# Score products of an attention stage on four 64x64 tiles of TensorE

## The chip, the cores and the metric

The kernel runs on one core of a Trainium2 chip. Its time is device time in microseconds (us) for the whole program. TensorE is called PE, VectorE DVE, ScalarE ACT, GpSimd POOL; SP is the queue that only issues DMAs. The program is written in a tile framework: it allots buffers from pools, puts the instructions of each engine into an order, and sets the semaphores between them.

## The reference

Four preactivation layers follow each other, each `x = x + f(group_norm(x))`. The change lies in the first, an axial attention over the 64 positions of one axis. With 4 images, 64 rows each, 16 groups of heads and 64 positions:

```
qkv = bn(einsum('nci,oc->noi', xp, w_qkv))          # n: image and row, i: position
q, k, v = qkv[:, :, :8], qkv[:, :, 8:16], qkv[:, :, 16:]      # per group g
qe = einsum('ngci,cij->ngij', q, q_emb)             # position terms of the query
ke = einsum('ngci,cij->ngij', k, k_emb)             # and of the key
qk = einsum('ngki,ngkj->ngij', qe, ke)              # their product: the scores
sim = bn(concat([qk, qe, ke]))                      # statistics over n, i, j
sim = softmax(sum of the three, axis=3)
out = einsum(sim, v), einsum(sim, v_emb) -> bn -> sum of the two
```

The batch norm of `sim` needs mean and variance of `qk`, `qe` and `ke` over all rows and positions before any softmax. Layers 2 to 4 are 3x3 convolutions (ternary weights; binary activations in two steps; weights built from a sigmoid form). They aren't touched.

## The kernel before

**Stage one** (L166 to L361) normalises the images, forms q, k and v (`po` at L284, `pv` at L299) and the sums for the first batch norm (`bn_stats` on DVE, squares on ACT, summed by PE in `psv`, L218). ACT copies q and k from PSUM into the two SBUF tiles `qs` of an image; after an image's last block, 16 DMAs on the SP queue (L326 to L331) write them to `q_d` in HBM.

**Stage two** (L389 to L667) makes the scores. It goes over 32 *pairs*: 4 images `b` times 8 pairs of groups `gp`. Before the loop, `et` is loaded on SP, and a chain of eight steps (`ptb` and `prs`, L410 to L414) makes the constants `tb` and `rsum` from it. Two pairs share one set `qb` (`projections(j)`: eight DMAs of 128 KB on SP; `scaled`: four DVE operations, L441). Each pair has two halves of its rows (`nb`), and each half two halves of the positions (`jh`). In one such quarter:

- `position_terms` (L466 to L486): 32 fp32 matmuls `pd` on eight 64x32 tiles (each matmul is two records in the profile, 64 for the block), into two PSUM buffers of `psd`; two DVE transposes (L483) bring them into the tiles `t0`, `t1`.
- `finish`, twice, for the half *before*: `product` (L488 to L504) does 16 fp32 matmuls `pq` of 64x64x64 on the tiles (0,0) and (64,64), into one PSUM bank; ACT copies it into the score tile `o` with a running sum (L499), then squares it in PSUM with another sum (L504). `finish` also issues the DMAs of the pair before (`qk_d`, on ACT's queue).

So a pair has four `pd` blocks and eight `product` calls of 32 records each. After each pair `term_sums` (L446 to L464) makes the statistics of `qe` and `ke`: three small DVE steps over q for the means (L451 to L453), four matmuls `ptq` (L456) and four DVE multiply-and-sum operations (L461) for the squares.

The pools set the order: `psd` has three buffers of two banks, which `pd` (two) and `ptq` (one) share; `psq` has two of one bank; `t0` and `t1` have two each, `o` two, `qb` five, loaded three ahead. Beside the pairs, ten weight jobs of later layers run, mostly on DVE: `weights_3` (L511 to L526) six times and `weights_2` (L528 to L553) four times; the framework puts them early in the stage. After the last pair, L601 to L608 finish the products and write the last scores, and L614 to L634 make the statistics from `acc` (products) and `esum` (terms).

**Stage three** (from L671) loads the scores back, applies the softmax and multiplies with v: `e` (L794), `exp` (L834), `pa` (L872), `den` (L845), `pe` (L897, 128x32 tiles). Its constants `vb` and `ve` are loaded on SP at its start. Then come the convolutions, with the chip's longest matmul lines (L993, L1284, L1378).

Of the kernel before, what the change touches and what calls it, by code (L numbers as in the profile page):

```python
# [18 lines left out]
P = 128  # L19
# [22 lines left out]
def network(ctx: ExitStack, tc, x, wqkv, relm, relt, relw, relv, counts, masks, vecs, rowv, ab, w1, l2w1, l2w2, l3w, mats, out):  # L42
# [10 lines left out]
    def scratch(name, shape):  # L53
        return dram.tile(shape, F32, name=name, tag=name)

    q_d = [scratch(f"q_d{b}", [GP, 8, 2, 2, 8, 512]) for b in range(B)]
    vt_d = [scratch(f"vt_d{b}", [4, 2, P, GP, 16, 8]) for b in range(B)]
    qk_d = [scratch(f"qk_d{b}", [GP, P, HW]) for b in range(B)]

# [106 lines left out]
    with ExitStack() as ph:  # L166
# [12 lines left out]
        st1 = sp.tile([P, 2, B * NB, 6], F32, name="st1")  # L179
        mx = sp.tile([P, 2, B], F32, name="mx")  # L180

        def normalised(b):
# [87 lines left out]
        for b in range(B):  # L270
            xs, gm, rs = ready
            qs = [qp.tile([P, 8, 8, 64], F32, name=f"qs{t}_{b}", tag="qs") for t in range(2)]
            for k in range(NB):
# [49 lines left out]
                if k in (3, 7) and 2 * b + k // 4 - 1 in range(len(pieces)):  # L323
                    i = 2 * b + k // 4 - 1
                    pieces_1[i] = weights_1(i, "wb")
            for t in range(2):  # L326
                for l in range(8):
                    nc.sync.dma_start(
                        out=q_d[b][:, l, t].rearrange("a r c f -> (r c) a f"),
                        in_=qs[t][:, EIGHT[l]].rearrange("p a h -> p (a h)"),  # L330
                    )  # L331
        while squares:
            add_squares()

        mv1 = small(sp, [P, 4, 2])
# [53 lines left out]
    with ExitStack() as ph:  # L389
        rp = pool(ph, "b_r")  # L390
        bqps += [pool(ph, f"b_q{i}") for i in range(3, 5)]
        tp_ = pool(ph, "b_t", 2)
        op = pool(ph, "b_o", 2)
# [8 lines left out]
        nc.sync.dma_start(out=rm, in_=relm)  # L402
        et = rp.tile([64, 8, P], F32, name="et")
        nc.sync.dma_start(out=et, in_=relt)
# [16 lines left out]
        sq = spread_scales(sp, psq, xs1, M_TKC, False, "pq")  # L421
        acc = sp.tile([P, 2, GP, B * 8], F32, name="acc")
        esum = sp.tile([P, 2, G, 2 * B], F32, name="esum")

        def projections(j):

            b, s = divmod(j, 4)
            q = bqps[j % 5].tile([P, 4, 8, 64], F32, name=f"qb_{j}", tag="qb")
# [17 lines left out]
        def term_sums(j, q, half):  # L446

            b, s = divmod(j, 4)
            gs, ks, col = slice(4 * s, 4 * s + 4), slice(4 * half, 4 * half + 4), 2 * b + half
            m = jp.tile([P, 4, 4], F32, name=f"m_{j}_{half}", tag="m")  # L450
            nc.vector.tensor_reduce(m, q[:, :, ks], AX.X, ALU.add)  # L451
            nc.vector.tensor_tensor(m, m, rsum[:, ks].unsqueeze(1).to_broadcast([P, 4, 4]), ALU.mult)
            nc.vector.tensor_reduce(esum[:, 0, gs, col], m, AX.X, ALU.add)  # L453
            ps = psd.tile([P, 4, 4, 64], F32, name=f"ptq_{j}_{half}", tag="pd")
# [4 lines left out]
            for g in range(4):  # L459
                junk = jp.tile([P, 4, 64], F32, name=f"pr_{j}_{half}_{g}", tag="pr")  # L460
                nc.vector.scalar_tensor_tensor(  # L461
                    junk, ps[:, :, g], 1.0, q[:, g, ks], ALU.mult, ALU.mult,
                    accum_out=esum[:, 1, 4 * s + g, col : col + 1],
                )  # L464

        def position_terms(q, ts, gp, nb, jh, name):  # L466
            pds = [psd.tile([P, 4, 32, 8], F32, name=f"pd_{name}_{t}_{jh}", tag="pd") for t in range(2)]
            for m in range(4):
                for g in range(2):
                    for kh in range(2):  # L470
                        for t in range(2):
                            rows = slice(64 * t, 64 * t + 64)
                            c = 2 * g + kh
                            a = 4 * kh + m
# [12 lines left out]

        def product(ts, o, k, col, gp, name):  # L488

            ps = psq.tile([P, 8, 64], F32, name=f"pq_{name}_{k}", tag="pq")  # L490
            for m in range(8):
                n = 8 * (k % 4) + m
                for g in range(2):
                    rows = slice(64 * g, 64 * g + 64)
                    nc.tensor.matmul(  # L495
                        ps[rows, m, :], lhsT=ts[1][rows, n // 2, :, n % 2], rhs=ts[0][rows, n // 2, :, n % 2],
                        start=True, stop=True, tile_position=(64 * g, 64 * g),
                    )
            nc.scalar.activation(  # L499
                o[:, :, 8 * k : 8 * k + 8, :], ps.rearrange("p n (a b) -> p a n b", b=2), AF.Copy,  # L500
                accum_out=acc[:, 0, gp, col : col + 1],
            )
            psf = ps.rearrange("p n i -> p (n i)")
            nc.scalar.activation(psf, psf, AF.Square, accum_out=acc[:, 1, gp, col : col + 1])  # L504

# [22 lines left out]
        def weights_2(i, g):  # L528

            w = kp.tile([P, 9, 64], F32, name=f"w2_{i}_{g}", tag="w2")  # L530
            if i == 0:
# [5 lines left out]
            w3 = w.rearrange("p k o -> p (k o)").rearrange("p (a n) -> p a n", a=3)  # L537
            u = kp.tile([P, 4, 3 * 64], F32, name=f"u2_{i}_{g}", tag="u2")
            t = kp.tile([P, 3 * 64], F32, name=f"t2_{i}_{g}", tag="t2")
# [20 lines left out]
        def finish(step, k):  # L560
            ts, o, b, gp, nb = step
            product(ts, o, 4 * nb + k, 8 * b + 4 * nb + k, gp, f"{b}_{gp}")

            if whole:
# [6 lines left out]
                if part == 3:  # L571
                    whole.pop()
            if nb == 1 and k == 3:
# [39 lines left out]
        tot = small(sp, [P, 2, GP])  # L613
        nc.vector.tensor_reduce(tot, acc, AX.X, ALU.add)  # L614
# [1203 lines left out]
```

## Time and profile before

| | |
|---|---|
| time, median of 3 runs | 2853.01 us (2845.20 to 2862.32) |
| time of the profiled execution | 2858.52 us |
| its span | 2856.7 us |
| PE busy | 2485.8 us (87%) |
| DVE busy | 1975.4 us (69%) |
| ACT busy | 1227.1 us (43%) |
| first `pd` of stage two | 287.3 us |
| last `pq` of stage two ends | 963.3 us |
| stage two's `pq`, busy over the whole span | 278.8 us, 8192 records |
| stage two's `pd`, likewise | 284.8 us, 8192 records |
| stage two's transposes, likewise | 304.1 us, 256 |

Busy time is an average over stages that are bound by different engines, so a stage has to be read from its own window. In a line of the groups, "128*32" or "64*64" is the part of the PE array that an instruction takes (rows x columns), the numbers behind it partitions x elements; "idle before" is what the engine waited ahead of this group, with the engine and line that ended the wait, and "issue" means that it waited for nothing that the profile shows. A PE record in the timeline overlaps the next, so paces are taken from start to start. PEld is the loading of a matmul's stationary operand, which runs beside PE.

### The profile page before, as it was taken

To read this page: it belongs to the slowest core of one execution; us is meant where nothing else is said; L and a number is where in the kernel's file an instruction comes from. 1 tells how busy PE (TensorE), PEld (TensorE's weight loads), DVE (VectorE), ACT (ScalarE), POOL (GpSimd) and SP (SyncE) were. 2 spreads that over 40 slices of the span, in tenths; PEclk is the share of its full clock that TensorE was granted. 3 is DMA by queue.
4 is the path that set the end of the run, shared out by engine and by line. 5 is a ranking of instruction groups with operands and counts; after the bars stand their busy time and mean duration, and the time that the engine had idled before them with its cause. 6 is when DMAs were issued, how large, how long until landed. Compare 5 with 4: busy or idle time off the path is not lost. (4 is left out here: it accounts for less than half of the span.)

```text
span 2856.7 us, 78236 instructions
## 1 busy us (share of the span) xinstructions
PE 2485.8 (87%) x34632; PEld 1675.3 (59%) x34632; DVE 1975.4 (69%) x3442; ACT 1227.1 (43%) x2240; POOL 96.3 (3%) x185
## 2 busy tenths in 40 slices
PE   7999889899999787888874789899998859999997
PEld 4566556667777566666764567677455424444443
DVE  6554997666666456666557878986888967958732
ACT  4554444555555555455533554653448521110100
POOL 0000000000000000000000000000000000000000
PEclk9999999999999799989997899999999979999998
DMA  6867466455544777777767546434436752333110
GB/s 241 256 204 217 137 192 161 126 128 130 145 109 104 181 255 258 263 255 248 258 216 231 167 165 198 163 132 171 132 116 242 279 196 92 118 117 134 45 45 31
DMA packets 257435, 489.71 MB, mean 171 GB/s; under 512 B 25984, under 2 KB 142336, under 8 KB 236352
## 3 DMA queue, kind: packets, MB, share of 16 engines
q1 hardware_dynamic: 184864, 292.32, 31.6%
q10 hardware_dynamic: 58336, 125.85, 15.8%
q0 software_dynamic: 13888, 66.46, 5.9%
q8 instruction: 274, 4.49, 0.6%
q14 instruction: 73, 0.60, 0.1%
HBM read 281.39 MB, written 203.16 MB: 170 GB/s over the span
## 5 line engine op out<-in xcount | busy, mean ns | idle before, releaser
L993 PE MATMUL gc<-gtr,g_u 128*128 128x512 f32 x1152 | 504.1, 599 | 13.8 <-DVE pc_o L1390 7.1
L993 PEld LDWEIGHTS gc<-gtr,g_u 128*128 128x128 f32 x1152 | 219.6, 192 | 290.1 <-issue 270.2
L483 DVE STREAM_TRANSPOSE t<-pd 128x1024 f32<-128x1024 f32 x256 | 304.1, 1226 | 114.6 <-PE pd L476 114.4
L476 PE MATMUL pd<-rm,qb 64*32 64x256 f32 x8192 | 284.8, 386 | 48.0 <-DVE t L483 41.3
L495 PEld LDWEIGHTS pq<-t,t 64*64 64x64 f32 x8192 | 259.1, 135 | 74.6 <-issue 50.8
L495 PE MATMUL pq<-t,t 64*64 64x64 f32 x8192 | 278.8, 220 | 18.7 <-issue 15.7
L499 ACT ACTIVATE o<-pq 128x512 f32<-128x512 f32 x256 | 152.1, 595 | 316.9 <-PE pq L495 311.2
L1378 PE MATMUL pc<-e_tr,e_k 128*64 128x512 bf16 x2304 | 264.9, 391 | 19.6 <-DVE e_tr L1367 13.0
L1284 PE MATMUL dc<-dh,d_u 128*128 128x512 f32 x768 | 235.3, 416 | 34.5 <-ACT dh L1261 34.5
L834 ACT ACTIVATE pt<-pt,sm 128x512 f32<-128x512 f32 x256 | 162.1, 709 | 170.8 <-DVE pt L804 170.7
L476 PEld LDWEIGHTS pd<-rm,qb 64*32 64x32 f32 x8192 | 157.0, 107 | 131.0 <-DVE t L483 59.6
L1284 PE MATMUL dc<-dl,d_u 128*128 128x512 f32 x768 | 230.7, 410 | 1.2 <-DVE dl L1262 1.1
L1378 PEld LDWEIGHTS <-e_k 128*64 128x64 bf16 x2304 | 144.9, 112 | 136.5 <-issue 27.4
L1284 PEld LDWEIGHTS dc<-dh,d_u 128*128 128x128 f32 x768 | 149.5, 196 | 75.8 <-ACT dh L1261 36.4
L804 DVE TENSOR_TENSOR pt<-e_False,si_False 128x1024 f32<-128x1024 f32 x128 | 151.6, 1216 | 35.1 <-PE e_False L794 34.0
L1284 PEld LDWEIGHTS dc<-dl,d_u 128*128 128x128 f32 x768 | 146.7, 193 | 43.6 <-DVE dl L1262 5.3
L1011 ACT COPY gc_c<-gc 128x512 f32<-128x512 f32 x32 | 18.6, 580 | 344.5 <-PE gc L993 324.5
L794 PE MATMUL e_False<-qc_False,rw 32*128 32x256 f32 x1024 | 129.7, 472 | 32.6 <-DVE pt L804 17.6
L504 ACT ACTIVATE pq<-pq 128x512 f32<-128x512 f32 x256 | 149.8, 585 | 3.9
L284 PE MATMUL po<-xg,wt 128*128 128x512 f32 x256 | 121.0, 611 | 6.5 <-DVE st L291 4.9
L299 PE MATMUL pv<-wt,xg 128*128 128x256 f32 x512 | 119.7, 382 | 0.0
L897 PE MATMUL pe_False<-pt,ve 128*32 128x64 f32 x4096 | 88.2, 238 | 34.5 <-issue 26.2
(396 smaller groups left out, 3611.0 us busy)
## 6 DMA issues: line engine op xcount, KB each, us to landing
si_False<-qk_d SPq DMA_DIRECT2D x64, 1024.0 KB
qk_d<-o ACTq DMA_DIRECT2D x124, 512.0 KB
x<-x_d SPq DMA_DIRECT2D x32, 1056.0 KB
xa<-in_x SPq DMA_DIRECT2D x16, 1024.0 KB
vt_d<-vs ACTq DMA_DIRECT2D x32, 512.0 KB
q_d<-qs SPq DMA_DIRECT2D x64, 256.0 KB
qb<-q_d SPq DMA_DIRECT2D x128, 128.0 KB
qc_False<-q_d SPq DMA_DIRECT2D x64, 256.0 KB
```

The source lines that it names most:

```text
L284: nc.tensor.matmul(psf, lhsT=wt[:, t, bass.ts(o, P)], rhs=xg[:, t, :], start=(t == 0), stop=(t == 1))
L476: nc.tensor.matmul(pds[t][32 * c : 32 * c + 32, m].rearrange("p j k -> p (j k)"), lhsT=q[rows, 2 * (gp % 2) + g, a, 32 * nb : 32 * nb + 32 ...
L483: nc.vector.transpose(ts[t][:, :, 32 * jh : 32 * jh + 32].rearrange("p a j b -> p j a b"), pds[t].rearrange("p m j k -> p j m k"),)
L495: nc.tensor.matmul(ps[rows, m, :], lhsT=ts[1][rows, n // 2, :, n % 2], rhs=ts[0][rows, n // 2, :, n % 2], start=True, stop=True, tile_posi ...
L499: nc.scalar.activation(o[:, :, 8 * k : 8 * k + 8, :], ps.rearrange("p n (a b) -> p a n b", b=2), AF.Copy, accum_out=acc[:, 0, gp, col : co ...
L504: nc.scalar.activation(psf, psf, AF.Square, accum_out=acc[:, 1, gp, col : col + 1])
L794: nc.tensor.matmul(es[x_ // 2][:, x_ % 2, :, :, par], lhsT=rw[rows, 63 - i : 127 - i].rearrange("p j r -> p (j r)"), rhs=q[rows, :, par, k ...
L804: nc.vector.tensor_tensor(dst, e, src, ALU.add)
L834: nc.scalar.activation(s, s, AF.Exp, scale=s2q[:, gp : gp + 1])
L993: nc.tensor.matmul(ms[k], lhsT=u[t][:, dx, k, bass.ts(co, P)], rhs=vs[t][:, k, :, dx : dx + 64], start=(first and dx == 0), stop=(last and ...
L1284: nc.tensor.matmul(at[k], lhsT=u[t][:, dx, k, bass.ts(co, P)], rhs=v[:, k, :, dx : dx + 64], start=(first and p_ == 0 and dx == 0), stop=( ...
L1378: nc.tensor.matmul(m[64 * g : 64 * g + 64], lhsT=parts[:, g, i, k, dx, :], rhs=vs[g][:, k, 8 * (q % 2) : 8 * (q % 2) + 8, dx : dx + 64], s ...
```

## The change

`product` now handles both halves of a pair's rows in one call and alternates between all four 64x64 tiles: half `nb` reads its terms from partitions 64*(g^nb) and writes its result to partitions 64*g, into a PSUM bank of its own. For that `position_terms` puts half 1 into exchanged partitions, and the products of a pair follow one whole pair behind its terms (`t0`, `t1` have four buffers each). A pair has four `product` calls of 64 records, each followed by two ACT copies out of PSUM and one ACT square over 128x1024, read from the score tile `o` in SBUF into a bf16 buffer that nobody reads. The three DVE steps for the q means leave `term_sums`. In their place, stage one sums each image's `qs` with two reductions over 128x4096, adds the four images up, and sends the result through HBM (`qs_d`: 16 DMAs on POOL's queue, four loads on SP) to a tile `qtot` of stage two; seven small DVE operations at the end of stage two turn it into the mean. `qb` has four buffers and is loaded two ahead; `et` and some tiles of the weight jobs share buffers now. The diff, cut:

```diff
+    qs_d = scratch("qs_d", [2, 8, 2, 8, GP, 8])
...
+        qsum = sp.tile([P, 2, B, 64], F32, name="qsum")
...
             for t in range(2):
+                nc.vector.tensor_reduce(qsum[:, t, b], qs[t].rearrange("p l a h -> p (l a) h"), AX.X, ALU.add)
+            for t in range(2):
                 for l in range(8):
                     nc.sync.dma_start(
                         out=q_d[b][:, l, t].rearrange("a r c f -> (r c) a f"),
...
+        qtot = small(sp, [P, 2, 8, 8])
+        nc.vector.tensor_reduce(
+            qtot.rearrange("p t l a -> p t (l a)"), qsum.rearrange("p t b x -> p t x b"), AX.X, ALU.add
+        )
+        for t in range(2):
+            for l in range(8):
+                nc.gpsimd.dma_start(
+                    out=qs_d[t, l].rearrange("r c a f -> (r c) a f"), in_=qtot[:, t, EIGHT[l]]
+                )
...
-        bqps += [pool(ph, f"b_q{i}") for i in range(3, 5)]
-        tp_ = pool(ph, "b_t", 2)
+        bqps += [pool(ph, "b_q3")]
+        tp_ = pool(ph, "b_t", 4)
...
-        et = rp.tile([64, 8, P], F32, name="et")
+        et = kp.tile([64, 8, P], F32, name="et", tag="u3")
...
-        acc = sp.tile([P, 2, GP, B * 8], F32, name="acc")
-        esum = sp.tile([P, 2, G, 2 * B], F32, name="esum")
+        acc = sp.tile([P, 2, 2, GP, B * 4], F32, name="acc")
+        esum = sp.tile([P, G, 2 * B], F32, name="esum")
+        qtot = sp.tile([P, 2, GP, 8], F32, name="qtot")
+
+        def load_sums():
+            for t in range(2):
+                for r in range(2):
+                    nc.sync.dma_start(
+                        out=qtot[64 * t : 64 * t + 64, r].rearrange("p a f -> p (a f)"),
+                        in_=qs_d[t, :, r].rearrange("l c a f -> l c (a f)"),
+                    )
...
-            m = jp.tile([P, 4, 4], F32, name=f"m_{j}_{half}", tag="m")
-            nc.vector.tensor_reduce(m, q[:, :, ks], AX.X, ALU.add)
-            nc.vector.tensor_tensor(m, m, rsum[:, ks].unsqueeze(1).to_broadcast([P, 4, 4]), ALU.mult)
-            nc.vector.tensor_reduce(esum[:, 0, gs, col], m, AX.X, ALU.add)
...
-                            c = 2 * g + kh
+                            c = 2 * (g ^ nb) + kh
...
-        def product(ts, o, k, col, gp, name):
-
-            ps = psq.tile([P, 8, 64], F32, name=f"pq_{name}_{k}", tag="pq")
+        def product(units, o, k, col, gp, name):
+
+            ps = [psq.tile([P, 8, 64], F32, name=f"pq_{name}_{k}_{nb}", tag="pq") for nb in range(2)]
             for m in range(8):
-                n = 8 * (k % 4) + m
-                for g in range(2):
-                    rows = slice(64 * g, 64 * g + 64)
-                    nc.tensor.matmul(
-                        ps[rows, m, :], lhsT=ts[1][rows, n // 2, :, n % 2], rhs=ts[0][rows, n // 2, :, n % 2],
-                        start=True, stop=True, tile_position=(64 * g, 64 * g),
-                    )
-            nc.scalar.activation(
-                o[:, :, 8 * k : 8 * k + 8, :], ps.rearrange("p n (a b) -> p a n b", b=2), AF.Copy,
-                accum_out=acc[:, 0, gp, col : col + 1],
-            )
-            psf = ps.rearrange("p n i -> p (n i)")
-            nc.scalar.activation(psf, psf, AF.Square, accum_out=acc[:, 1, gp, col : col + 1])
+                n = 8 * k + m
+                for nb, ts in enumerate(units):
+                    for g in range(2):
+                        src = 64 * (g ^ nb)
+                        rows = slice(src, src + 64)
+                        nc.tensor.matmul(
+                            ps[nb][64 * g : 64 * g + 64, m, :], lhsT=ts[1][rows, n // 2, :, n % 2],
+                            rhs=ts[0][rows, n // 2, :, n % 2], start=True, stop=True, tile_position=(src, 64 * g),
+                        )
+            for nb in range(2):
+                n = 32 * nb + 8 * k
+                nc.scalar.activation(
+                    o[:, :, n : n + 8, :], ps[nb].rearrange("p n (a b) -> p a n b", b=2), AF.Copy,
+                    accum_out=acc[:, 0, nb, gp, col : col + 1],
+                )
+            part = o.rearrange("p a (x n) b -> p a x (n b)", x=2)[:, :, :, 16 * k : 16 * k + 16]
+            junk = jp.tile([P, 32, 2, 16], BF16, name=f"sq_{name}_{k}", tag="sq", bufs=1)
+            nc.scalar.activation(junk, part, AF.Square, accum_out=acc[:, 1, 0, gp, col : col + 1])
...
-            w = kp.tile([P, 9, 64], F32, name=f"w2_{i}_{g}", tag="w2")
+            w = kp.tile([P, 9, 64], F32, name=f"w2_{i}_{g}", tag="w3")
...
-            u = kp.tile([P, 4, 3 * 64], F32, name=f"u2_{i}_{g}", tag="u2")
+            u = kp.tile([P, 4, 3 * 64], F32, name=f"u2_{i}_{g}", tag="ew")
...
-            parts = kp.tile([P, 3, 4 * 3 * 64], BF16, name=f"k2_{i}_{g}", tag="k2")
+            parts = kp.tile([P, 3, 4 * 3 * 64], BF16, name=f"k2_{i}_{g}", tag="u3")
...
-        qs = [projections(j) for j in range(3)]
+        qs = [projections(j) for j in range(2)]
+        load_sums()
         scaled(0, qs[0])
...
-                if gp % 2 == 0 and j + 3 < 4 * B:
-                    qs.append(projections(j + 3))
+                if gp % 2 == 0 and j + 2 < 4 * B:
+                    qs.append(projections(j + 2))
...
+                units = []
                 for nb in range(2):
                     ts = [tp_.tile([P, 16, 64, 2], F32, name=f"t{t}_{b}_{gp}_{nb}", tag=f"t{t}") for t in range(2)]
+                    units.append(ts)
                     for jh in range(2):
                         position_terms(q, ts, gp, nb, jh, f"{b}_{gp}_{nb}")
                         if last is not None:
-                            finish(last, 2 * jh)
-                            finish(last, 2 * jh + 1)
-                    last = (ts, o, b, gp, nb)
+                            finish(last, 2 * nb + jh)
+                last = (units, o, b, gp)
...
+        nc.vector.tensor_tensor(acc[:, 0, 0], acc[:, 0, 0], acc[:, 0, 1], ALU.add)
+        nc.vector.tensor_reduce(tot, acc[:, :, 0], AX.X, ALU.add)
         tot_e = small(sp, [P, 2, G])
-        nc.vector.tensor_reduce(tot_e, esum, AX.X, ALU.add)
+        nc.vector.tensor_reduce(tot_e[:, 1], esum, AX.X, ALU.add)
+        nc.vector.tensor_tensor(
+            qtot, qtot, rsum.unsqueeze(1).unsqueeze(1).to_broadcast([P, 2, GP, 8]), ALU.mult
+        )
...
```

More of the change, by code (lines that the diff above doesn't have):

```diff
@@ L421, in network @@
         sq = spread_scales(sp, psq, xs1, M_TKC, False, "pq")
-        acc = sp.tile([P, 2, GP, B * 8], F32, name="acc")
-        esum = sp.tile([P, 2, G, 2 * B], F32, name="esum")
+        acc = sp.tile([P, 2, 2, GP, B * 4], F32, name="acc")
[8 more added lines that the diff above has]
+                    )
         def projections(j):
             b, s = divmod(j, 4)
-            q = bqps[j % 5].tile([P, 4, 8, 64], F32, name=f"qb_{j}", tag="qb")
+            q = bqps[j % 4].tile([P, 4, 8, 64], F32, name=f"qb_{j}", tag="qb")
             for t in range(2):
@@ L448, in term_sums @@
             b, s = divmod(j, 4)
-            gs, ks, col = slice(4 * s, 4 * s + 4), slice(4 * half, 4 * half + 4), 2 * b + half
-            m = jp.tile([P, 4, 4], F32, name=f"m_{j}_{half}", tag="m")
-            nc.vector.tensor_reduce(m, q[:, :, ks], AX.X, ALU.add)
-            nc.vector.tensor_tensor(m, m, rsum[:, ks].unsqueeze(1).to_broadcast([P, 4, 4]), ALU.mult)
-            nc.vector.tensor_reduce(esum[:, 0, gs, col], m, AX.X, ALU.add)
+            ks, col = slice(4 * half, 4 * half + 4), 2 * b + half
             ps = psd.tile([P, 4, 4, 64], F32, name=f"ptq_{j}_{half}", tag="pd")
@@ L462, in term_sums @@
                     junk, ps[:, :, g], 1.0, q[:, g, ks], ALU.mult, ALU.mult,
-                    accum_out=esum[:, 1, 4 * s + g, col : col + 1],
+                    accum_out=esum[:, 4 * s + g, col : col + 1],
                 )
@@ L560, in finish @@
         def finish(step, k):
-            ts, o, b, gp, nb = step
-            product(ts, o, 4 * nb + k, 8 * b + 4 * nb + k, gp, f"{b}_{gp}")
+            units, o, b, gp = step
+            product(units, o, k, 4 * b + k, gp, f"{b}_{gp}")
             if whole:
@@ L572, in finish @@
                     whole.pop()
-            if nb == 1 and k == 3:
+            if k == 3:
                 whole.append((b, gp, o, 0))
         last = None
-        qs = [projections(j) for j in range(3)]
+        qs = [projections(j) for j in range(2)]
+        load_sums()
         scaled(0, qs[0])
@@ L613, in network @@
         tot = small(sp, [P, 2, GP])
-        nc.vector.tensor_reduce(tot, acc, AX.X, ALU.add)
+        nc.vector.tensor_tensor(acc[:, 0, 0], acc[:, 0, 0], acc[:, 0, 1], ALU.add)
+        nc.vector.tensor_reduce(tot, acc[:, :, 0], AX.X, ALU.add)
         tot_e = small(sp, [P, 2, G])
-        nc.vector.tensor_reduce(tot_e, esum, AX.X, ALU.add)
+        nc.vector.tensor_reduce(tot_e[:, 1], esum, AX.X, ALU.add)
+        nc.vector.tensor_tensor(
+            qtot, qtot, rsum.unsqueeze(1).unsqueeze(1).to_broadcast([P, 2, GP, 8]), ALU.mult
+        )
+        first = small(sp, [P, 2, GP])
+        nc.vector.tensor_reduce(first, qtot, AX.X, ALU.add)
+        nc.vector.tensor_tensor(
+            first, first, sq[:, 0].rearrange("p (a r) -> p r a", r=2), ALU.mult
+        )
+        every = small(sp, [P, 1])
+        nc.vector.tensor_reduce(every, rsum, AX.X, ALU.add)
+        nc.vector.tensor_scalar(every, every, float(B * 64), None, ALU.mult)
+        nc.vector.scalar_tensor_tensor(
+            tot_e[:, 0].rearrange("p (a r) -> p r a", r=2), sq[:, 1].rearrange("p (a r) -> p r a", r=2),
+            every, first, ALU.mult, ALU.add,
+        )
         each = float(P) / (B * 64 * 64 * 64)
```

## The prediction

> **What bounds the kernel now.** The page lists `pd` (L476) and `pq` (L495), the matmuls of stage two, among its costliest groups; the timeline puts that stage between the first `pd` at 287.3 us and the end of the last `pq` at 963.3. So I read busy time by windows first. Columns: window, PE, PE weight loads, VectorE (DVE), ScalarE (ACT), GpSimd, granted PE clock, DMA share, GB/s.
>
> ```profile
> 300.00:350.00 50.00, 41.46 (x1067) 30.09 (x1064) 50.00 (x97) 24.25 (x74) 1.63 (x3) 0.97 0.41 119
> ...
> 400.00:450.00 50.00, 42.90 (x1084) 31.01 (x1070) 48.87 (x95) 22.65 (x70) 3.23 (x6) 0.97 0.76 222
> 450.00:500.00 50.00, 46.84 (x1302) 35.78 (x1298) 32.79 (x56) 25.91 (x80) 0.00 (x0) 1.00 0.60 156
> ...
> 700.00:750.00 50.00, 44.18 (x1236) 33.49 (x1234) 33.98 (x59) 24.33 (x75) 0.00 (x0) 1.00 0.48 119
> ```
>
> There are two phases. Up to about 460 us DVE never rests: the weight jobs (L511 to L553) share it with the pairs. From there to the end PE is the full engine, and DVE and ACT have a third and a half free. The groups of 500 to 900 us give the price list of the second phase (busy us, mean ns, idle before and its releaser):
>
> ```profile
> L483 DVE STREAM_TRANSPOSE t<-pd 128x1024 f32<-128x1024 f32 x160 | 190.5, 1229 | 88.3 <-PE pd L476 88.1
> L495 PE MATMUL pq<-t,t 64*64 64x64 f32 x5120 | 174.4, 220 | 15.1 <-issue 12.5 <-ACT pq L504 2.6
> L476 PE MATMUL pd<-rm,qb 64*32 64x256 f32 x5118 | 166.7, 379 | 15.7 <-DVE t L483 11.9 <-issue 3.8
> ...
> L499 ACT ACTIVATE o<-pq 128x512 f32<-128x512 f32 x160 | 95.1, 595 | 189.8 <-PE pq L495 187.4 <-issue 2.5
> ...
> L504 ACT ACTIVATE pq<-pq 128x512 f32<-128x512 f32 x160 | 93.7, 585 | 2.5
> L456 PE MATMUL ptq<-qb,tb 128*128 128x256 f32 x160 | 39.9, 392 | 0.7 <-DVE t L483 0.7
> ...
> L461 DVE SCALAR_TENSOR_TENSOR pr<-ptq,qb 128x256 f32<-128x256 f32 x80 | 29.2, 421 | 47.2 <-PE ptq L456 47.2
> L451 DVE TENSOR_REDUCE m<-qb 128x16 f32<-128x1024 f32 x20 | 24.3, 1214 | 0.3
> L441 DVE TENSOR_SCALAR qb<-qb,sm 128x512 f32<-128x512 f32 x41 | 19.7, 542 | 0.0
> ```
>
> 160 transposes are 20 pairs of eight, so a pair takes 400/20 = 20.0 us. DVE and ACT wait for PE. The PE timeline shows a pair's inside (start, us, ..., records):
>
> ```profile
> 708.43 2.14 PE L495 MATMUL pq<-t,t 64*64 64x64 f32 x64
> 710.50 1.96 PE L476 MATMUL pd<-rm,qb 64*32 64x256 f32 x64
> 712.38 2.14 PE L495 MATMUL pq<-t,t 64*64 64x64 f32 x64
> ...
> 719.97 1.99 PE L456 MATMUL ptq<-qb,tb 128*128 128x256 f32 x8
> 721.89 1.48 PE L476 MATMUL pd<-rm,qb 64*32 64x256 f32 x41
> ```
>
> From start to start: 64 `pq` records 2.07 us (32.3 ns each), 64 `pd` records 1.88 us (29.4), 8 `ptq` records 1.92 us. Four of each of the first two and one `ptq`: 4 x 3.95 + 1.92 = 17.7 us; the waits in the table add (15.1 + 15.7 + 0.7)/20 = 1.6; 0.7 stays unexplained.
>
> `pq` runs on two of the four 64x64 tiles: 64.6 ns per record and tile. Stage three has fp32 matmuls with the same 64 moving columns, spread over four tiles (L897, 128x32):
>
> ```profile
> 1126.31 1.08 PE L845 MATMUL den_False<-pt,cnt 128*32 128x128 f32 x32
> 1127.21 1.11 PE L897 MATMUL pe_False<-pt,ve 128*32 128x64 f32 x64
> 1128.26 1.66 PE L794 MATMUL e_False<-qc_False,rw 32*128 32x256 f32 x16
> ```
>
> 64 records in 1.05 us: 16.4 ns each, 65.6 per tile. So a tile sets its own pace, and issue is no limit at 16.4 ns. But L897 loads 32 weight columns a record (1.95 columns per ns), `pq` 64: today's `pq` also loads 64/32.3 = 1.98. That coincidence carries the main rival. L794 loads 128 columns every 50 ns or so: 2.6 columns per ns.
>
> **What the Trainium skill says.** "TensorEngine Tiling (Array Packing)", Key Properties: tiles work independently, loads and matmuls of different tiles side by side; the L897 pace agrees. The same page, PSUM Bottleneck: after such a speed-up the evacuation may become the bound; I find that here below. "TensorE: Matmul & The Clock Gate", Part 3: a weight load overlaps matmuls in flight only where the row group differs. L897's tiles all span the same 128 rows and still run at 16.4 ns, so the trace disagrees; if it held, half of the new order's neighbours share a row group.
>
> **The change part by part.**
>
> *Four tiles.* The 64 `pq` records of a block take 64 x 16.4 = 1.05 us where the L897 pace holds (at L794's load rate 64 x 25 = 1.60). PE per pair: 4 x (1.88 + 1.05) + 1.92 = 13.6 us. PE is then no longer the bound. `psd` has three buffers and a `pd` block takes two, so the next block waits for the first transpose of the one before: 1.88 (`pd`) + 0.16 (release) + 1.19 (transpose) + 0.08 = 3.31 us; the `pq` fits into the 1.43 between. At 1.60 a block is 3.48, so the gain hardly depends on where in 16 to 25 ns it lands. `ptq` follows the fourth `pq`: 1.05 + 1.92 - 1.43 adds 1.54, making 14.8 us. In every second pair the four scalings (L441, 1.92 us together) stand ahead of the first transposes and show by about 1.4: 16.2. Mean 15.5, plus 0.8 of "issue" gaps ((12.5 + 3.8)/20; as many instructions as before): **16.3 us against 20.0**.
>
> *Squares.* Per block ACT now has two copies at 0.72 (595 ns and most of the accumulator read) and one square of 128x1024 from SBUF, not two of 128x512. Its price is bounded by 1054 ns (L1189, 128x1024 fp32 to bf16 with a sum) and 2 x 585 plus a read; I take 1.2. ACT: 2.6 to 2.9 us in a block of 3.31. It hides under DVE and PE; uncovered, as behind the last pair, it shows: four blocks at ACT's pace, about 10 us in place of about 5: +5.
>
> *The q sums.* Three DVE operations leave each pair (1.21 + 0.17 + 0.16, about 1.4 of 13.3 us DVE). In phase two DVE had slack; in phase one DVE is the clock. The weight jobs cost about 90 us DVE. Before: 7 pairs x 13.3 + 90 = 183 us. After: 8 x 11.9 + 90 = 185 us: one pair more in the same time, so 24 pairs are left where 25 were. The sums go to stage one as eight reduces of 128x4096 (L451 has 1.2 us for 1024 elements, so about 4.7 each, 38 in all). Stage one is PE's, with PE 50.0 of 50 us and DVE some 40% idle: hidden; bounds 0 and +8, where a reduce holds up a group-norm step once. I take +1.
>
> *Queues at the start.* In the new order on SP's queue the load of `et` stands behind the 16 `q_d` writes (1.01 us each, 267 to 283). The `ptb` chain, eight steps of 1.17 us that began at 275.4, therefore begins at about 286. Also, DVE has the multiplication of `qtot` ahead of the first transpose, and `qtot` makes a round trip: 16 GpSimd DMAs (issue 0.55 each at L526, up to 1.0 as on SP) and four SP loads. Everything on DVE is queued behind it, and the first `pd` blocks wait for their buffers. First transposes at about 303 in place of 291.5. As phase one needs DVE for work and not for order, only DVE's idle counts: bounds +2 and +15, I take +6.
>
> *Buffers.* Projections go from five buffers to four and from three ahead to two; a set of eight loads lands within the 32 us of two pairs, so nothing. Shared tags in the weight jobs: GpSimd's first load of L532, at 259.5 us before, comes after five of the other jobs and behind the sixteen small writes; DVE has pair work meanwhile: nothing, at worst one job's 5 us, which falls into phase two's slack.
>
> *The end.* Today the second `qk_d` write (L604) is issued at 973.7, held by the load of `ve`, which was issued after the last product sums. In the new order `ve` no longer waits for those: 0 to -9 us; I take 0.
>
> *Sum.* Start 290.7 + 185 + 6 + 1 = 483; + 24 x 16.3 = 391: 874; + 5 tail: 879, less whatever the end gives, against 963: **-84 us**. The profiled execution took 2858.5 us (span 2856.7), which makes 2775; the median, 2853.0, lies 5.5 lower (its runs span 2845 to 2862) and would give 2769. I name 2771.
>
> **The rivals.**
>
> *Loads share one path (1).* If all tiles' loads together pass about 2 columns per ns, L897 and today's `pq` both sit at it and four tiles give nothing; L794's 2.6 speaks against. Half-way, 28.5 ns: block 1.88 + 1.82 = 3.70, pair 4 x 3.70 + 1.92 + 1.2 = 17.9, x 24 = 430: end at 918, saves 45: 2808.
>
> *No gain on PE (2).* 32 ns as today: pairs at 20.0, end at 483 + 480 = 963: 2853.
>
> *Slower (3).* `pq` as in (2), and the `qtot` round trip (scattered pieces of 32 bytes, writes and then reads through HBM) holds DVE's queue 15 to 25 us rather than 6, with nothing behind it that could run: 2853 + 9 to 19, about 2868. It decides only if `pq` gains under 2.5 ns a record (64 x 4 x 24 x 2.5 = 15 us). The trace has no such round trip; the writes' issue on SP, 16 in 16.2 us, speaks for some of it.
>
> *Better (4).* The `ve` hold disappears, and issue gaps fall into the wait for transposes: -9 and -0.8 x 24 = -19: 2743.
>
> **How the numbers follow.** Main case 58% (2771, own range 2750 to 2795), rival 1 20% (2795 to 2830), rival 2 9% (2840 to 2866), rival 3 5%, rival 4 8%. The range 2744 to 2828 leaves out rivals 2 and 3 and the edges of 1 and 4, under 20%. This kernel's measurement tells about 0.5% (14 us) from no change: faster 0.87, same 0.08, slower 0.05.
>
> **What would show it.** Right: `pq` blocks of 64 records in 1.05 to 1.6 us; from 500 us on DVE busy at 36 or more of 50 with `pd` waiting for the transposes; eight transposes per 16.3 us; ACT near 33 of 50 (8 x 0.72 + 4 x 1.2 in 16.3 us); last `pq` near 875. Wrong: `pq` at 28 ns or more with PE still at 45 of 50 (rivals 1 and 2); a DVE gap of over 10 us before 310 (rival 3); ACT never waiting for `pq` (my square is too cheap).

## The result, and the profile after

The change takes 2833.6 us in the median of 20 runs, the kernel before 2857.5 in its 20: a ratio of 0.992, interval [0.9903, 0.9937]. That is a gain of 0.8% where 2.9% was forecast, and 2834 lies above the range. The profiled execution, the shortest of the 20, took 2822.3 us (span 2820.4).

Busy time by windows, kernel after (columns as before):

```profile
300.00:350.00 50.00, 39.77 (x922) 23.92 (x930) 49.81 (x100) 13.80 (x36) 1.08 (x2) 0.88 0.19 60
400.00:450.00 50.00, 32.53 (x912) 21.00 (x896) 39.10 (x74) 19.50 (x50) 3.34 (x6) 0.88 0.74 224
450.00:500.00 50.00, 41.53 (x1281) 27.46 (x1284) 37.66 (x59) 22.90 (x60) 2.73 (x5) 0.88 0.57 169
...
700.00:750.00 50.00, 43.35 (x1333) 29.26 (x1322) 30.17 (x46) 25.91 (x65) 0.00 (x0) 0.97 0.42 113
```

From 700 to 750 us no engine is full: PE 43, DVE 30, ACT 26 of 50. DVE at 36 or more was to show the forecast right. The groups of 500 to 900 us, kernel after:

```profile
L502 DVE STREAM_TRANSPOSE t<-pd 128x1024 f32<-128x1024 f32 x174 | 207.4, 1230 | 120.8 <-PE pd L495 120.8
L495 PE MATMUL pd<-rm,qb 64*32 64x256 f32 x5531 | 203.1, 384 | 35.1 <-issue 22.6 <-DVE t L502 12.2
L516 PE MATMUL pq<-t,t 64*64 64x64 f32 x5532 | 113.1, 224 | 18.2 <-issue 13.0 <-ACT o L522 4.6
...
L522 ACT ACTIVATE o<-pq 128x512 f32<-128x512 f32 x174 | 102.3, 594 | 159.5 <-PE pq L516 155.7 <-PE pd L495 2.1 <-issue 1.6
...
L528 ACT ACTIVATE sq<-o 128x1024 bf16<-128x1024 f32 x86 | 90.9, 1057 | 33.1 <-DMA qb<-q_d 30.6
```

174 transposes are 21.75 pairs in 400 us: 18.4 us a pair, not 16.3. `pq` fell from 174.4 us for 20 pairs to 113.1 for 21.75. DVE waits for `pd` 120.8 us, more than the 88.1 of before, though the transposes were to become the bound. What grew is PE's "issue": 22.6 + 13.0 = 35.6 us, 1.64 a pair, against 0.8 before. The PE timeline, kernel after, shows what such a gap is:

```profile
672.57 1.96 PE L495 MATMUL pd<-rm,qb 64*32 64x256 f32 x64
674.46 1.19 PE L516 MATMUL pq<-t,t 64*64 64x64 f32 x64
675.58 2.30 PE L495 MATMUL pd<-rm,qb 64*32 64x256 f32 x64
677.81 0.51 PE L516 MATMUL pq<-t,t 64*64 64x64 f32 x17
679.44 0.95 PE L516 MATMUL pq<-t,t 64*64 64x64 f32 x47 [1.12 <-issue]
680.32 1.96 PE L495 MATMUL pd<-rm,qb 64*32 64x256 f32 x64
```

The undisturbed `pq` block takes 1.12 us from start to start, near the 1.05 of the forecast. The next one stops after 17 of its 64 records, in the midst of a block, where no buffer is asked for, and PE waits 1.12 us for nothing that the groups or the timeline name.

The trace's DMA packets name it. PE's instructions arrive on the DMA queue q8, in packets of 16 KB. The page of the kernel after counts them for the whole kernel (packets, MB, share):

```profile
q8 instruction: 273, 4.47, 0.6%
```

A packet holds 128 matmul records with their weight loads: in e2 below 8192 more records take 64 more packets. Between 500 and 900 us PE has 41 "issue" waits in the kernel after (the 35.6 us), and every one of them ends 1.16 to 1.58 us after the landing of a packet; the 16 of the kernel before (16.3 us) end 1.22 to 1.57 us after one. So at these stops PE waits for its next instructions.

At stage three's first matmul the change is 22.7 us ahead (962.7 us in place of 985.4, profiled executions). The starts of `ptq`, a pair's last PE step, show where (parts rounded): the first `ptq` starts at 317.0 us in place of 304.7 (+12.3); first to tenth takes 208.6 in place of 211.8 (-3.2); tenth to 32nd 409.5 in place of 439.2 (-29.6, 18.61 us a pair in place of 19.96); from there to stage three's first matmul 27.6 in place of 29.7 (-2.1). Behind that point another 13.6 us separate the two executions. The kernel's text is the same there, and the single profiles of all kernels here take from 1848 to 1875 us for it, so this part isn't put down to the change.

### The profile page after: what moved, and what is told of

It is laid out like the page before. It is cut to its first block, busy times and chain, and to the rows that moved or that the text cites. A ratio compares the mean times of both kernels' runs of the same rounds, so it can differ in the third digit from the quotient of the medians.

```text
span 2820.4 us, 77670 instructions
## 1 busy us (share of the span) xinstructions
PE 2410.9 (85%) x34632; PEld 1575.9 (56%) x34632; DVE 1968.3 (70%) x3362; ACT 1202.5 (43%) x1984; POOL 105.2 (4%) x201
## 4 chain that ended last, share of the span: by engine, by line
issue 24%; PE 18%; DVE 9%; DMA 8%; ACT 4%; POOL 0%; SPq 0%; DVEq 0%; POOLq 0%; ACTq 0%
PE dc L1326 8%; DMA at_d<-o_False 3%; PE e_False L836 2%; PE pe_False L939 2%; DMA x<-x_d 2%; PE pr_False L905 2%; PE pc L1420 2%; PE den_False L887 2%; PE pa_False L914 1%; DVE pt L846 1%; DVE e_tr L1409 1%; DMA dx<-in_x 1%; DMA z_d<-dx 1%; DVE o_False L923 1%; DMA qc_False<-q_d 1%
## 5 line engine op out<-in xcount | busy, mean ns | idle before, releaser
L495 PE MATMUL pd<-rm,qb 64*32 64x256 f32 x8192 | 318.1, 399 | 77.8 <-DVE t L502 49.6
L1420 PE MATMUL pc<-e_tr,e_k 128*64 128x512 bf16 x2304 | 262.5, 388 | 16.6 <-DVE e_tr L1409 10.2
L495 PEld LDWEIGHTS pd<-rm,qb 64*32 64x32 f32 x8192 | 169.3, 110 | 178.8 <-DVE t L502 72.6
L876 ACT ACTIVATE pt<-pt,sm 128x512 f32<-128x512 f32 x256 | 162.1, 709 | 174.4 <-DVE pt L846 156.6
L1420 PEld LDWEIGHTS <-e_k 128*64 128x64 bf16 x2304 | 143.1, 112 | 133.0 <-issue 22.6
L516 PEld LDWEIGHTS pq<-t,t 64*64 64x64 f32 x8192 | 148.6, 140 | 94.6 <-issue 78.6
L516 PE MATMUL pq<-t,t 64*64 64x64 f32 x8192 | 172.1, 227 | 32.0 <-issue 25.4
L1053 ACT COPY gc_c<-gc 128x512 f32<-128x512 f32 x32 | 18.6, 581 | 344.6 <-PE gc L1035 344.6
L836 PE MATMUL e_False<-qc_False,rw 32*128 32x256 f32 x1024 | 134.2, 485 | 29.6 <-DVE pt L846 15.3
L528 ACT ACTIVATE sq<-o 128x1024 bf16<-128x1024 f32 x128 | 135.3, 1057 | 47.3 <-DMA qb<-q_d 43.7
```

The source lines that it names most:

```text
L495: nc.tensor.matmul(pds[t][32 * c : 32 * c + 32, m].rearrange("p j k -> p (j k)"), lhsT=q[rows, 2 * (gp % 2) + g, a, 32 * nb : 32 * nb + 32 ...
L516: nc.tensor.matmul(ps[nb][64 * g : 64 * g + 64, m, :], lhsT=ts[1][rows, n // 2, :, n % 2], rhs=ts[0][rows, n // 2, :, n % 2], start=True, ...
L528: nc.scalar.activation(junk, part, AF.Square, accum_out=acc[:, 1, 0, gp, col : col + 1])
L836: nc.tensor.matmul(es[x_ // 2][:, x_ % 2, :, :, par], lhsT=rw[rows, 63 - i : 127 - i].rearrange("p j r -> p (j r)"), rhs=q[rows, :, par, k ...
L876: nc.scalar.activation(s, s, AF.Exp, scale=s2q[:, gp : gp + 1])
L1420: nc.tensor.matmul(m[64 * g : 64 * g + 64], lhsT=parts[:, g, i, k, dx, :], rhs=vs[g][:, k, 8 * (q % 2) : 8 * (q % 2) + 8, dx : dx + 64], s ...
```

## The experiments

Each is an edit of the kernel after, except two of the kernel before. "A pair" is the mean from the tenth `ptq` to the 32nd in that run's timeline. Theory 1 says that PE's supply of instructions, fetched in packets of 16 KB, holds the pair. Theory 2 says that ACT's queue does, since the `qk_d` writes in it wait for `qb` loads. Theory 3 is the forecast's own bound, transposes and buffers, with jitter. In the expectations a "lane" is a semaphore that counts the landings of DMAs; in the trace of after, `qb` loads and `qk_d` writes wait on the same ones (semaphores 104 to 107, for instance).

### e1 and e5: half as many `pd` matmuls

```diff
-            for m in range(4):
+            for m in (0, 2):
...
-                            w = 56 - 8 * a + 32 * jh
+                            w = 56 - 8 * a
...
-                                pds[t][32 * c : 32 * c + 32, m].rearrange("p j k -> p (j k)"),
+                                pds[t][32 * c : 32 * c + 32, m : m + 2].rearrange("p m j k -> p (m j k)"),
...
-                                rhs=rm[rows, w : w + 32, :].rearrange("p j k -> p (j k)"),
+                                rhs=rm[rows, w : w + 64, :].rearrange("p j k -> p (j k)"),
```

> The changed kernel, but each pd matmul covers 512 moving columns where it covered 256, so that a pd block has 16 matmuls (32 records) and not 32 (64); the columns streamed, the PSUM written and the transposes are the same, the values of the terms are wrong. Records in a pair: 392 in place of 520. Theory 1 (the supply of PE instructions, one 16 KB fetch for each 128 records, about 3.4 to 3.75 us a fetch, holds the pair at 18.7 us): the supply then allows 11.5 us, the transposes and psd buffers set the pace, a pair takes 15.5 to 16.5 us after 500 us, and the kernel gains 45 to 60 us on the changed one. Theory 2 (ACT's queue held by the qk_d writes) and theory 3 (transposes and buffers with their jitter): 18 us or more, gain under 15 us.

> The kernel before, with its pd matmuls merged as in the first experiment (512 moving columns, 392 records in a pair; the values of the terms are wrong). Theory 1: before, PE's work (17.7 us a pair from its paces) and its instruction supply (4.06 fetches of about 3.5 us, 14.2 us) are well apart, so only the issue gaps and part of the waits go: a pair at 18.5 to 19.5 us in place of 20.0, 10 to 35 us gained, less than the 50 us that the same edit gave the changed kernel. Rival (merging makes pd itself faster, whatever the supply): a gain of 50 us or more here too.

e1: 2784.1 us, 0.9755 [0.9732, 0.9778] of before, 50 us under the change; a pair at 16.97; 36 us of the gain lie between the tenth `ptq` and the 32nd, 14 between the first and the tenth. e5: 2817.0, 0.9869 [0.9835, 0.9904]; a pair at 18.75, most of them 17.7 and 19.6 in turn. The groups of 500 to 850 us in e1:

```profile
L502 DVE STREAM_TRANSPOSE t<-pd 128x1024 f32<-128x1024 f32 x167 | 198.8, 1228 | 85.9 <-PE pd L495 85.9
L495 PE MATMUL pd<-rm,qb 64*32 64x512 f32 x2657 | 190.5, 603 | 6.4 <-DVE t L502 6.2 <-issue 0.2
L516 PE MATMUL pq<-t,t 64*64 64x64 f32 x5315 | 104.3, 223 | 18.7 <-ACT o L522 12.4 <-issue 6.3
```

"Issue" ahead of `pd` is gone (0.2 us). In place of 273 instruction packets for the whole kernel there are 241, as this line of e1's queues on its page says (packets, MB, share):

```profile
q8 instruction: 241, 3.95, 0.6%
```

PE streamed as many columns as before, and the pair still lost 1.6 us: theory 1 holds, theory 3 alone does not. Pairs 26 to 30, behind the last `qb` loads, take 16.2 and 14.9 us in turn, the two values that the forecast worked out. The kernel before gained 38 us, just over what was expected and under the rival's 50: it too was held, by less. The totals alone would leave the rival, that merged matmuls are faster in themselves. The timelines don't: an undisturbed `pd` block takes 1.88 to 1.89 us from start to start in all four kernels, merged or not.

### e2 and e9: twice as many

```diff
+                for part in range(2):
...
-                            w = 56 - 8 * a + 32 * jh
+                                w = 56 - 8 * a + 32 * jh + 16 * part
...
-                                rhs=rm[rows, w : w + 32, :].rearrange("p j k -> p (j k)"),
+                                    rhs=rm[rows, w : w + 16, :].rearrange("p j k -> p (j k)"),
```

> The opposite: each pd matmul of 256 columns is split into two of 128, so that a block has 128 records of half the length; values and streamed columns as in the changed kernel. Records in a pair: 776. Theory 1: 6.06 fetches of 3.4 to 3.75 us, a pair takes 21 to 23 us, the kernel loses 60 to 100 us. Theories 2 and 3: a block of 128 records can pass in 1.9 us (14.7 ns a record, a pace the trace shows elsewhere), a pair stays at 18 to 19 us, within 15 us of the changed kernel.

> The kernel before, with its pd matmuls split as in the second experiment (776 records in a pair in place of 520). Theory 1 in its strong form: the supply alone sets the pace at 776 records, so two tiles or four make no difference, and a pair takes about 26 us as it did there (25 to 27.5). Rival (the four-tile order or the later products cause what the split showed): 20 to 22.5 us.

One run each: 3026.1 and 3049.5 us, a pair at 26.1 and 26.6. The direction is theory 1's; the loss is 190 us, not 60 to 100. The packets start 4.28 us apart in the mean in e2, not 3.4 to 3.75, and PE's granted clock is 0.88 there from 500 to 900 us (0.99 in the change); how much of the excess is due to which is open. Two tiles or four, the pair is nearly the same. Groups of 500 to 900 us in e2:

```profile
L496 PE MATMUL pd<-rm,qb 64*32 64x128 f32 x7819 | 172.4, 308 | 64.3 <-issue 60.7 <-DVE t L503 3.4
L503 DVE STREAM_TRANSPOSE t<-pd 128x1024 f32<-128x1024 f32 x122 | 145.3, 1229 | 196.7 <-PE pd L496 196.7
...
L517 PE MATMUL pq<-t,t 64*64 64x64 f32 x3904 | 91.2, 240 | 50.7 <-issue 50.6
```

`pd` and `pq` wait 111 us of 400 for "issue" and 3.4 for transposes, and DVE waits 196.7 us for `pd`: PE is held by how many instructions it gets.

### e3 and e7: ACT's queue

e3 issues the `qb` loads on GpSimd's queue, e7 the `qk_d` writes on SP's:

```diff
-                    nc.sync.dma_start(
+                    nc.gpsimd.dma_start(
                         out=q[64 * t : 64 * t + 64, g].rearrange("p a n -> p (a n)"),
```
```diff
-                nc.scalar.dma_start(
+                nc.sync.dma_start(
                     out=qk_d[wb][wgp].rearrange("(j r) f -> r j f", r=2)[part % 2][:, bass.ts(part // 2, HW // 2)],
```

> The changed kernel, with the qb loads issued on the GpSimd queue in place of SP's, so that they no longer share completion lanes with the qk_d writes on ACT's queue. Theory 2: ACT's waits of 3.8 us ahead of the first square of every second pair vanish, and with them 1 to 1.9 us a pair: 25 to 45 us gained. Theory 1: the waits vanish, but PE was held by its instruction supply: 0 to 12 us gained.

> The changed kernel, with the qk_d writes issued on SP's queue, so that their waits for the qb loads' lanes no longer stand in ACT's queue. Theory 2: ACT's 3.8 us waits in every second pair go, and 10 to 40 us with them. Theory 1 (these waits fall into the time that PE is held by its supply): a pair stays within 0.5 us of 18.6, under 12 us either way.

e3: 2870.0 us, 1.0022 [1.0001, 1.0043] of before: 36 us lost, which neither theory expected. ACT's waits for the loads went, and pairs with loads take 23.6 to 25.2 us up to the 25th, those without 16.6 to 19. Waits of 500 to 850 us in e3 (total, times, longest):

```profile
PE pd L495 <- issue: 41.7, 18, 5.9
PE pq L516 <- issue: 23.3, 14, 6.2
```

In the trace of one such pair PE goes on with a new packet at 665.0 us and the next packet's transfer starts 7.0 us later, after GpSimd's eight issues (659.9 to 664.3); the median over all stops is 1.2 us. Between 580 and 840 us this happens seven times, each time around the end of such a set of issues (5.3 to 7.1 us). So instruction packets can be late, and then PE stands; that it is GpSimd's issuing that delays them fits in time, but isn't shown.

e7: 2837.5 us, 0.992 [0.9891, 0.9949], a pair at 18.68. ACT's waits for loads are gone, the time is that of the change: theory 2 falls. (In the profiles of e7 and e11 the first ten pairs take 9 and 11 us longer than in the change and in e1, so the writes may cost time on SP too; one profile each doesn't settle it.)

### e11: both holds off

The edits of e1 and e7 together.

> The changed kernel, with the merged pd matmuls (wrong values of the terms) and the qk_d writes on SP's queue. In the first experiment pairs took 16.2 us in turn with 17.9, and 14.9 once no more qb loads were issued. If ACT's wait for a load's lane makes that difference: all pairs at 14.9 and 16.2 in turn, 15.6 in the mean, ACT without waits of 3 to 4 us. If not: 16.8 to 17.2 as there.

One run, 2775.0 us; a pair at 16.22, between the two expectations; the pairs with loads, 17.9 us in e1, take 15.8 here. ACT's waits of 500 to 850 us in e1:

```profile
ACT o L522 <- PE pq L516: 114.8, 69, 4.2
ACT sq L528 <- DMA qb<-q_d: 33.3, 8, 5.1
```

and in e11:

```profile
ACT o L522 <- PE pq L516: 137.6, 89, 2.7
```

So ACT's hold is real and costs 0.7 us a pair (one profile each) once PE's supply no longer covers it.

### e6: two tiles in the changed kernel

```diff
-            for m in range(8):
-                n = 8 * k + m
-                for nb, ts in enumerate(units):
+            for nb, ts in enumerate(units):
+                for m in range(8):
+                    n = 8 * k + m
                     for g in range(2):
```

> The changed kernel, with the 64 records of a product in the order of their half: all of half 0, then all of half 1, so that two tiles work at a time as before; everything else as in the change. If the four tiles are what the change lives from: a pq block of 2.0 to 2.1 us and a pair of 19.5 to 20.5 us, 20 to 40 us lost on the changed kernel, which makes it as slow as the kernel before or slower by up to 15 us. Rival (the instruction supply sets the pace in both): a pair at 18.6 to 19 us, under 10 us lost.

2848.5 us, 0.9986 [0.9968, 1.0005]: 15 us lost, between the two. Groups of 500 to 900 us in e6:

```profile
L495 PE MATMUL pd<-rm,qb 64*32 64x256 f32 x5402 | 183.3, 381 | 15.1 <-issue 12.4 <-DVE t L502 2.4
L516 PE MATMUL pq<-t,t 64*64 64x64 f32 x5376 | 168.4, 222 | 4.8 <-issue 3.5 <-ACT o L522 1.0
```

An undisturbed `pq` block takes 1.89 us here (2.07 in the kernel before, 1.12 in the change), and `pq` is busy 55 us more in this window than in the change. But a pair grows from 18.61 only to 19.03: of the time that `pq` gives back with four tiles, about 20 us turn into "issue" (15.9 us here, 35.6 there) and 13 into waits for transposes and copies (3.4 here, 16.8 there).

### e4, e8 and e12: the weight jobs and the start

```diff
-            w = kp.tile([P, 9, 64], F32, name=f"w2_{i}_{g}", tag="w3")
+            w = kp.tile([P, 9, 64], F32, name=f"w2_{i}_{g}", tag="w2")
```
```diff
-        et = kp.tile([64, 8, P], F32, name="et", tag="u3")
+        et = rp.tile([64, 8, P], F32, name="et")
...
-                junk = jp.tile([P, 4, 64], F32, name=f"pr_{j}_{half}_{g}", tag="pr")
+                junk = jp.tile([P, 4, 64], F32, name=f"pr_{j}_{half}_{g}", tag="pr", bufs=1)
```

(In e8 and e12 `weights_2` also adds in place, which frees the tile `t2`.)

> The changed kernel, with a buffer of its own again for the loads of weights_2 (in the change they share the tag of weights_3's products). Theory: DVE's first step of weights_2 waits for a load that can't start before the buffer is free, and transposes queue behind it (9.4 us of DVE waits between 400 and 500 us, pairs of 27.4 and 26.8 us there): 12 to 25 us gained. Rival: DVE was full in that phase anyway and the work is only put off: under 5 us.

> The changed kernel, with a buffer of its own for et (room made by one buffer less for an unread result and by an addition done in place), so that its load goes ahead of the sixteen q_d writes again. First transposes at 291 to 296 us in place of 305, no stretch at half PE clock from 274 to 305, 7 to 14 us gained. Rival (the stage's first pairs are bound by DVE's work, not by their start): under 4 us.

> The eighth experiment once more with more rounds, as the one version so far that is faster than the change and computes the same: 2815 to 2826 us, 8 to 18 us under the changed kernel, if its earlier result holds; 2829 to 2837 if it was chance.

e4: 2839.6 us, 0.9947 [0.9914, 0.9981], no gain; first to tenth `ptq` 206.0 us in place of 208.6. In these single profiles the shared buffer costs 3 us at most. e8: 2819.6, 0.9893 [0.9851, 0.9935]; e12: 2816.6, 0.9862 [0.9838, 0.9887]: 14 and 17 us under the change, and the fastest kernel here that leaves the computation as it is. The first `ptq` starts 8.7 and 7.0 us earlier, the first transposes at 297.3 and 300.2 us, later than the 291 to 296 expected. What the start cost the changed kernel (its timeline):

```profile
288.38 0.76 PE L424 MATMUL ptb<-et 64*128 64x128 f32 x2 [9.03 <-DMA et<-in_relt]
```

PE stood 9.0 us for `et`. From 274 to 305 us its granted clock was 0.51 (e8: 0.65, so that stretch was shortened, not gone; before: 0.72), and the first `pd` blocks ran at about 54 ns a record. At stage three's first matmul 4.1 (e8) and 8.6 us (e12) of the earlier start are left in the profiles; the rest of the gain isn't located.

### e10 and e13: where and when the packets end

e10 adds 64 records ahead of the pairs, e13 leaves out the `qb` loads after the fourth.

```diff
+        for i in range(32):
+            ps = psq.tile([P, 1], F32, name=f"fill_{i}", tag="pq")
+            nc.tensor.matmul(ps, lhsT=et[:, i % 8, :], rhs=mt[0:64, M_ALL, 0:1], start=True, stop=True)
```
```diff
-                    qs.append(projections(j + 2))
+                    qs.append(projections(j + 2) if j < 2 else qs[j - 2])
```

> The changed kernel, with 32 small matmuls (64 records) added ahead of the pairs, whose results nobody reads. They move the places at which a fetch of 16 KB ends by half a cycle of 128 records. In the changed kernel the pairs with that place inside pd (7 to 13 and 21 to 27) take 18 to 22 us, those with it inside pq (13 to 20 and 27 to 32) 17 to 18. If the place of the fetch decides: the two stretches change their roles, so pairs 14 to 20 take 18.5 us or more and pairs 21 to 26 under 18.3. If the slow stretches belong to the work (other loads, other images): pairs 21 to 26 stay the slow ones at 19 to 20.5.

> The changed kernel without the qb loads after the fourth: later pairs take the buffers of earlier ones again, so the terms have wrong values, and the instructions of all engines but SP stay as they are. Open: PE's gaps at the end of a fetched 16 KB are 0.4 to 0.6 us in some pairs and 1.5 to 4 us in others, with qb loads under way in every second pair. If the loads' traffic is what makes fetches late: a pair at 17.2 to 17.8 us in the mean after 500 us, with no gap over 2 us. If not: 18.3 to 18.8 with gaps as before.

Means, with the place of the packets' ends as the gaps show it:

```
                    pairs                     ends in pq    ends in pd
after               14-20 / 21-26               17.9          19.4
e10                 21-26 / 14-20               19.1          18.7
e13                 14-22 / 23-28               17.8          18.7
```

e10 (2837.7 us, one run; a pair at 19.06) is a miss: pairs 14 to 20 became slower, as expected, but 21 to 26 hardly faster; its slow pairs are those with loads under way (19.3 to 22.6 against 16.8 to 18.2 in 21 to 26). In e13 (one run) the second expectation came true: a pair at 18.29, gaps up to 3.5 us from start to start, and 37.6 us of "issue" between 500 and 900 us (35.6 in the change). So the loads' traffic isn't what makes the stops; it may account for 0.3 us a pair and for outliers. (e13's total, 2807.5 us, says little: from stage three's first matmul on its profile is the shortest of all, 1848.4 us.) That pairs take about 0.9 us more where a packet ends inside `pd` is seen in e13, but e10 has it the other way round: the role of the place isn't shown.

## Why the prediction was wrong

The failed step is one term of the pair's sum: "plus 0.8 of "issue" gaps ((12.5 + 3.8)/20; as many instructions as before)", with the sentence it rests on, that "issue is no limit at 16.4 ns". That was read from a burst of 64 records. From record starts in the trace of before, the fastest 64 records anywhere took 14.5 ns each, the fastest 256 already 21.8 and the fastest 512 27.0: a burst draws on what has been fetched. A block of the changed kernel, 128 records in the forecast's 3.31 us, asks for 25.9 ns, for pairs on end. In the trace of after (500 to 900 us) PE goes on 1.37 us after a packet has landed (1.26 to 1.51 in eight of ten), the next packet starts about 1.2 us after that, and takes 0.96: about 3.5 us for each packet of some 128 records, longer than the block. As many instructions in less time made the gaps larger, not equal.

With its size: counted as idle time, the stops grew from 0.8 us a pair to 1.64. Counted from start to start, as the forecast's paces are, they cost about 1.0 us a pair before and 2.3 in the change (estimates from the record starts of 500 to 900 us, against the usual distance at the same place of a block). The forecast's 16.3 was 13.6 for PE's paces, 1.9 for transposes, scalings and buffers, and 0.8 for "issue". The 18.6 measured are about 14.0 (4 x (1.89 + 1.12) + 1.92), 2.3 for "issue" and 2.3 for everything else. So 1.5 of the 2.3 us missing are this term, and the rest is spread over the others. The granted clock isn't the cause: 0.99 from 500 to 900 us, and 1.00 before.

The Trainium skill has this in "Runtime: NRT & Kernel Launch", Instruction fetch mechanics: blocks of 16 KiB, 256 instructions, and a crossing that is "mostly hidden". The packet size agrees with the page (274 packets, 4.49 MB, before). "Mostly hidden" does not hold here: 35.6 us of "issue" waits in 400, and 50 us gained with fewer matmuls.

Point by point:

- **Four tiles.** Right: `pq` at 1.12 us a block against 1.05. Rival 1 falls.
- **The pair.** 14.8 and 16.2 us without supply limits were right (e1, pairs 26 to 30: 14.9 and 16.2), 16.3 in all was not: 18.6. That e11's mean of 16.22 meets the 16.3 is chance: e11 has half the `pd` matmuls and no hold of ACT. From the eighth `ptq` at 485.3 us (forecast: 483) the 24 pairs to the 32nd took 449.8 us and not 391. This is 59 us of the miss.
- **The start.** First transposes at 305.2 us (forecast 303), eight pairs at the time foreseen; that DVE's idle alone counts was right as a sum. That the PE clock would be halved from 274 to 305 us was not foreseen.
- **Phase one.** Right as a sum for the change, but "one pair more in the same time" was not: the kernel before itself starts its eighth `ptq` at 477.2 us, where 7 pairs were reckoned to end at about 474 (290.7 + 183). From the first `ptq` to the eighth the change saves 4.2 us (168.3 in place of 172.5). That this didn't spoil the total is luck: the total used the sum for the change only. The buffers costed at nothing cost 3 us at most (e4).
- **The squares.** 1057 ns and a read of 187: 1.24 against 1.2. ACT 26 to 28 of 50, since pairs are longer.
- **Tail and end.** From the last `ptq` to the end of `pq` 11.8 us in place of 7.6 (+4.2, forecast +5); from there to stage three 15.9 in place of 22.2 (-6.3; forecast 0, bound -9).
- **ACT's queue.** That the `qk_d` writes would wait there for `qb` loads was missed: hidden behind the supply in the change (e7), 0.7 us a pair without it (e11).

Open: a pair holds about 4.06 packets, 14.2 us at 3.5, and takes 18.6, so the supply doesn't set the whole pair's pace: it stops PE inside the dense blocks, and waits for transposes and copies come on top. Why some packets start 2 to 4 us after PE goes on, and not 1.2, isn't settled (loads under way: e3, e10, hardly in e13).

## What to carry to other kernels

A faster engine step that keeps its number of instructions raises the demand on the instruction supply; work out nanoseconds per instruction over more than one packet of instructions, not over a burst, and look for the fastest such stretch in the trace. Over 2048 records the fastest stretch of all kernels here has 29.9 ns a record (e2); the forecast's 16.3 us for 520 records asked for 31.3. Where "issue" waits stand inside blocks and at an even distance, see whether they end just after an instruction packet lands. Here, where they did, fewer and longer instructions gained more than faster ones: halving one kind of matmul was worth 50 us (with wrong values of the terms; no kernel here has that gain with the right ones), doubling the tiles in another about 15. A constant that shares a buffer to save space can move its load behind a queue of writes and hold up the start of a stage (here by 7.0 to 8.7 us).

## What the runs showed of the hardware that was not expected

PE's instructions came in 16 KB packets, one for each 128 matmul records or so. The shortest time from the start of one packet to that of the next in all 15 profiles is 3.09 us (e3), and in the change the usual distance after a stop was about 3.5 us. With 776 records a pair the pace was 33.6 ns a record, with 520 in the change 35.8, with 392 hardly set by it (0.2 us of "issue" ahead of `pd`). Issuing 128 KB loads from GpSimd in place of SP went with instruction packets that started up to 7.1 us after PE had gone on, in place of about 1.2, and cost 36 us. In the change PE stood from 279.0 to 288.4 us, and its granted clock was 0.51 from 274 to 305 us (0.72 before).
